# Macaron S4D block on one core: the last two SSM batches made in two parts, by position

## Chip, cores and metric

One core of a Trainium2 chip runs the whole kernel. The metric is device time in microseconds (us) of one execution; the comparison is with the kernel before on the same chip.

## The reference

Input `x` is 8 sequences of 2048 positions with 256 features, all in float32. Three sublayers follow one another:

```python
x = x + 0.5 * ffn(layernorm(x), w1, b1, w2, b2)          # sublayer a
x = x + attn(layernorm(x), ...)                          # the SSM
x = x + 0.5 * ffn(layernorm(x), w1, b1, w2, b2)          # sublayer b, same weights

def ffn(x, w1, b1, w2, b2):       # 256 -> 1024 -> 256
    return relu(x @ w1 + b1) @ w2 + b2

def attn(x, ...):                 # S4D, 256 channels, 64 complex states each
    K = 2 * real(einsum('hn,hnl->hl', Ct, exp(dtA * l)))  # a kernel of 2048 lags
    y = irfft(rfft(x, 2 * L) * rfft(K, 2 * L))[:L]        # causal convolution
    r = x + y + x * D
    return layernorm(r) * ln_w + ln_b
```

## The kernel before

**Tiles.** A sequence is cut into 16 chunks of 128 positions; 8 sequences times 16 chunks are 128 columns (chunk and sequence). The feed-forward sublayers take them two columns at a time, as 64 groups of 256 tokens. After sublayer a the normalized rows lie in one large buffer, `u`, with four quarters `q` of 32 columns each and 256 channels in each quarter. The outputs of the SSM are written back into the same buffer, seen through the view `uo`.

**The SSM.** The convolution is done chunk by chunk: a state per channel, carried from chunk to chunk. The 256 channels are 32 batches of 8 (`bt`), and the batches form ten groups (`PLAN`, L1026) of 2, 4 or 4 batches, whose states lie in one of three buffers, `xsE`, `xsA` and `xsB`. They share their places with the weights: `xsA` with the first weights (tag `wA`), `xsB` with the second (`wB`), `xsE` with tag `wE`. `states` (L1055) makes the chunks' states with the `pt` tables (PE products `pv`, copied out by ACT), `whole` (L1234) carries them over the chunks on DVE, and `outputs` (L1122) makes the rows of a batch:

- SP loads two lag tables `tz` from `kpad` (L1129) and two P tables `ot` (L1147), 256 KB each. Their places rotate by tag, `TZS` and `OTS` (L1034, L1035): even batches in `xl` and `xh`, odd ones in `pl`, `hx`, and the buffer `xn`. For the last group there is a second rotation, in which half of the even batch's tables lie in `x`.
- ACT gathers the batch's channels out of `u` into two tiles `uc` (L1136, tag `hx`).
- PE makes `uc` times `tz` (L1152, 8 products, 16 records in the profile) and the states times `ot` (L1161, 16 products on half the rows each, 32 records), both into two PSUM banks `py`, one for the even and one for the odd channels.
- ACT copies both banks into `uo` (L1167); for the last batch DVE copies the second.

The main loop (L1267) makes a group's outputs and then the states of the group three further on. The last group (`xsE`) holds batches 30 and 31.

**The weights again.** Sublayer a's weights are overwritten by the states, so `again` (L1238) loads them once more for sublayer b: `wb1` as 8 transfers of 256 KB, `wb2` as 4 of 512 KB, on SP. The first four of `wb1` are written down after batch 30's outputs, the others after batch 31's. Each is pinned behind the instruction written just ahead of it on its engine.

**Sublayer b.** `sublayer` (L875) runs over half slots `t`, from -19 on. For t below 0, ACT and DVE keep the order in which the code writes their instructions; after that the library's scheduler orders them by its own estimate, as it does for PE and SP throughout, except where an instruction is pinned. A step of `t` lets each running generator go on to its next `yield`. Each half slot has one block of `up` (PE products `ph`, L856, 6 records), one ReLU on ACT (L928), one difference on DVE (L116) and, three half slots later, one block of `down` (PE products `po`, L866, 6 records). Eight half slots are a group. `pre_b` (L1286) makes a group's input: SP loads `xb`, the rows kept in DRAM (L1293, tag `x`, five places); POOL adds the norm's biases `lnb_sb` (L1294); DVE takes the statistics of the SSM rows (`st_r`), writes (row - mean) times weight into `ys`, scales it and adds it to `xb`; `ffn_in` (L752) takes the statistics again, normalizes into `xn`, transposes (on PE for the first two groups, by DMA for the rest) and splits into `xh` (ACT) and `xl` (DVE). The first groups use the columns of the last quarter, the fourth, and go downwards from there. `post_b` (L1314) adds the result to `xb` on DVE (L1316) and SP stores 256 KB (L1319).

**PSUM banks** (L106): four of tag `h` (`py`, `ph`), two `o` (`pv`, `po`), one `t` and one `b`. SBUF places (L107):

```python
BUFS = {"e": 1, "te": 1, "x": 5, "xh": 2, "xl": 2, "hx": 4, "pl": 2, "g": 1, "gt": 1}
```

Of the kernel before, what the change touches and what calls it, by code (L numbers as in the profile page):

```python
# [10 lines left out]
F32 = mybir.dt.float32  # L11
# [8 lines left out]
P = 128  # L20
# [23 lines left out]
def macaron_s4d_kernel(  # L44
# [17 lines left out]
    nc = tc.nc  # L62
    V = nc.vector
    A_ = nc.scalar
    G_ = nc.gpsimd

    B, L, H = x.shape
    N = c_re.shape[1]
    W = w1.shape[1]
    NJ = L // P  # L70
    CB = (NJ - 1) * B
    NQ = 4
# [3 lines left out]
    NTB = 2  # L76
    TOK = NTB * P
    NG = NJ * B // NTB
# [14 lines left out]
    BCH = 8  # L93
    NBT = H // BCH
    HCH = BCH // 2
    PB = BCH // 2
    KROW = 256
# [6 lines left out]
    wpool = ctx.enter_context(tc.tile_pool(name="wpool", bufs=1))  # L104
# [4 lines left out]
    def bank(tag, name):  # L109
        return ps.tile([P, 512], F32, name=name, tag=tag, bufs=BANKS[tag])  # L110

    def slot(tag, shape, name, dtype=F32):
        return work.tile(shape, dtype, name=name, tag=tag, bufs=BUFS[tag])
# [12 lines left out]
    CQ = JQ * B  # L126
    u = upool.tile([P, NQ, H, CQ], F32, name="u")


    uo = u.rearrange("p q (b h) m -> p q b (h m)", h=8).rearrange("p q b (m h) -> p q b m h", h=8)  # L130
# [84 lines left out]
    o_dram = [dram.tile([P, BCH * P], F32, name=f"o_{i}") for i in range(NBT)]  # L215
    pv_dram = [dram.tile([P, 2 * BCH * P], U16, name=f"pv_{i}") for i in range(2)]
    pt_dram = [dram.tile([P, BCH * P], F32, name=f"pt_{i}") for i in range(NBT)]
    kpad = dram.tile([H, KROW], F32, name="kpad")
# [470 lines left out]
    def stats(srcs, name, pin=False, mv=None):  # L689
        st = stat.tile([P, NTB, 6], F32, name=f"st_{name}", tag="st")  # L690
        mv = moments(NTB, name) if mv is None else mv
        for i, src in enumerate(srcs):
            ins = V.bn_stats(st[:, i, :], src)
            if pin:
                tc.keep_in_program_order(ins)
        for i in range(NTB):
            V.bn_aggr(mv[:, i, :], st[:, i, :])
        return mv
# [329 lines left out]
    sizes = [p[2] - p[1] for p in PLAN]  # L1028
# [2 lines left out]
    SPAN = {"A": 16, "B": 16, "E": 8}  # L1031
    TAGS = ("e", "te")
    LASTX = len(PLAN) - 1
    OTS = ("xh", "xh", "pl", None), ("xh", "x", "pl", None)  # L1034
    TZS = ("xl", "xl", "pl", "hx"), ("xl", "x", "pl", "hx")  # L1035
    xbuf = {}

    def states_of(gr):
        key, at, end = PLAN[gr]
        if key not in xbuf:  # L1040
            t = wpool.tile([P, 2, SPAN[key], NJ * B], F32, name=f"xs{key}", tag=f"w{key}")
            G_.memset(t[:, :, :, 0:B], 0.0)
            xbuf[key] = t
        return xbuf[key][:, :, at:end]

    def batches(gr):
        for p0 in range(0, sizes[gr], PB):
            yield p0, (starts[gr] + p0) // PB
# [54 lines left out]
    def scan(gr, E, p0, p1, j0, j1, tags):  # L1103
# [7 lines left out]
        for j in range(j0, j1):  # L1111
# [7 lines left out]
            E.tensor_add(xv[:, :, :, j + 1, :], xv[:, :, :, j + 1, :], t2)  # L1119
            yield  # L1120

    def outputs(gr, p0, bt):  # L1122
        xs = states_of(gr)
        py, tzs, ucs, ots = [], [], [], []
        for c in range(2):
            tz = slot(TZS[gr >= LASTX][(2 * bt + c) % 4], [P, PB, P], f"tz{bt}_{c}")

            row = kpad[BCH * bt + c, 1:]
            nc.sync.dma_start(  # L1129
                out=tz,  # L1130
                in_=bass.AP(row.tensor, row.offset, [[1, P], [2 * KROW, PB], [1, P]]),
            )
            tzs.append(tz)

            uc = slot("hx", [P, PB, P], f"uc{bt}_{c}")
            A_.copy(  # L1136
                uc.rearrange("p l (q m) -> p l q m", q=NQ),
                u[:, :, BCH * bt + c : BCH * (bt + 1) : 2, :].rearrange("p q l m -> p l q m"),
            )
            ucs.append(uc)  # L1140
        for ri in range(2):
            tag = OTS[gr >= LASTX][(2 * bt + ri) % 4]
            ot = (
                slot(tag, [P, PB, P], f"ot{bt}_{ri}") if tag
                else xn.rearrange("p i (l m) -> p (i l) m", m=P)
            )
            nc.sync.dma_start(out=ot, in_=o_dram[bt][:, ri * PB * P : (ri + 1) * PB * P])  # L1147
            ots.append(ot)
        for c in range(2):
            py.append(bank("h", f"py{bt}_{c}").rearrange("p (l m) -> p l m", l=PB))  # L1150
            for l in range(PB):
                nc.tensor.matmul(  # L1152
                    py[c][:, l, :], ucs[c][:, l, :], tzs[c][:, l, :],
                    start=(l == 0), stop=False, skip_group_check=True,
                )

        for l in range(PB):
            for ri in range(2):
                for c in range(2):
                    cs = slice(c * N, (c + 1) * N)  # L1160
                    nc.tensor.matmul(  # L1161
                        py[c][:, l, :], xs[cs, ri, p0 + l, :], ots[ri][cs, l, :],
                        start=False, stop=(l == PB - 1 and ri == 1), skip_group_check=True,
                    )
        for c in range(2):

            (V.tensor_copy if bt == NBT - 1 and c else A_.copy)(  # L1167
                uo[:, :, bt, :, c::2], py[c].rearrange("p l (q m) -> p q m l", q=NQ)
            )

    def some(j0, j1):

        if (j1 - j0) % JQ == 0:
            return u[:, j0 // JQ : j1 // JQ]
        q = j0 // JQ
        return u[:, q : q + 1, :, (j0 - q * JQ) * B : (j1 - q * JQ) * B]
# [57 lines left out]
    def whole(gr):  # L1234
        for _ in scan(gr, V, 0, sizes[gr], 1, NJ - 1, TAGS):
            pass

    def again():  # L1238

        wb1 = wpool.tile([P, 2, NDC, W], F32R, name="wb1", tag="wA")  # L1240
        for f in range(0, W, W // 4):
            fs = slice(f, f + W // 4)
            for i in range(2):
                tc.keep_in_program_order(
                    nc.sync.dma_start(out=wb1[:, i, :, fs].bitcast(F32), in_=w1_dram[i][:, :, fs])
                )
            if f == W // 4:
                yield
        wb2 = wpool.tile([P, 2, NFC, H], F32R, name="wb2", tag="wB")
        for f in range(0, NFC, 4):  # L1250
            fs = slice(f, f + 4)
            for i in range(2):
                tc.keep_in_program_order(
                    nc.sync.dma_start(out=wb2[:, i, fs].bitcast(F32), in_=w2_dram[i][:, fs])
                )
        yield wb1, wb2

    reload = again()

    for _ in head:  # L1260
        pass
# [1 line left out]
    for _ in states(2):  # L1263
        pass
    whole(2)
    for gr in range(len(sizes)):
        for p0, bt in batches(gr):  # L1267
            outputs(gr, p0, bt)
            if bt == NBT - 2:
                next(reload)  # L1270
        if gr + AHEAD < len(sizes):
            for _ in states(gr + AHEAD):
                pass
            whole(gr + AHEAD)
    wb1, wb2 = next(reload)

    G_.memset(xn[:, :, H - 1 : H], 1.0)
    ys = wpool.tile([P, 2, NTB, H], F32, name="ys", tag="wE")


    lnw_sb = slot("e", [P, H], "lnw_sb")
# [4 lines left out]
    def pre_b(g):  # L1286
        by_dma = g >= DMA_B

        for _ in range(0 if by_dma else (3, 5)[g]):
            yield  # L1290
        xt = xts[g] = slot("x", [P, NTB, H], f"xb_{g}")
        i0 = g * NTB
        nc.sync.dma_start(out=xt, in_=x1_dram[i0 : i0 + NTB].rearrange("i m h -> m i h"))  # L1293
        G_.tensor_add(xt, xt, lnb_sb.unsqueeze(1).to_broadcast([P, NTB, H]))  # L1294
        uc = [uo[:, i // CQ, :, i % CQ] for i in range(P - 1 - i0, P - 1 - i0 - NTB, -1)]
        mv = stats(uc, f"r{g}", PIN & 2)
        yield
        s = root(mv, f"r{g}")
        yield
        y = ys[:, g % 2]  # L1300
        for i in range(NTB):
            yb, lb = (t.rearrange("p (b h) -> p b h", h=BCH) for t in (y[:, i, :], lnw_sb))
            stt(yb, uc[i], mv[:, i, 0:1], lb, ALU.subtract, ALU.mult)
        yield
        rs = rstds(mv, s, f"r{g}")
        yield
        for i in range(NTB):
            ins = stt(xt[:, i, :], y[:, i, :], rs[:, i : i + 1], xt[:, i, :], ALU.mult, ALU.add)
            if PIN & 1:
                tc.keep_in_program_order(ins)  # L1310
        yield
        return (yield from ffn_in(xt, f"b{g}", NTB if g else 1, by_dma))

    def post_b(g, po):  # L1314
        xt = xts.pop(g)
        V.tensor_add(xt, po, xt)  # L1316
        yield
        rows = out[0, g * NTB]
        nc.sync.dma_start(  # L1319
            out=bass.AP(rows.tensor, rows.offset, [[P * H, NJ], [L * H, B], [1, NTB * H]]),  # L1320
            in_=xt.rearrange("p i h -> p (i h)"),
        )

    sublayer(
        [wb1[:, i] for i in range(2)], [wb2[:, i] for i in range(2)], pre_b, post_b, 19, "b"
    )


# [30 lines left out]
```

## Time and profile before

| | |
|---|---|
| median of 3 runs | 1771.14 us (1767.55 to 1773.35) |
| the profiled execution | 1773.44 us |
| its span, first to last instruction | 1771.7 us |
| PE busy | 1728.3 us, 98% of the span |
| DVE busy | 1370.2 us, 77% |
| ACT busy | 997.8 us, 56% |
| POOL busy | 592.8 us, 33% |
| mean granted clock of PE | 0.993 |
| last product of the SSM to first `ph_b` | 1017.2 to 1026.4 us |
| last product of sublayer b | 1767.0 us |

In the profile's lines a time is the start and the number after it the length, in us. `[0.70 <-DMA ot<-o]` says that the engine had stood idle for 0.70 us before the instruction, and that the one that ended it was the transfer of `ot`. PE is TensorE's products and PEld its weight loads, which overlap; DVE is VectorE, ACT ScalarE, POOL GpSimd, and SPq the queue on which SP issues transfers. `py<-tz,uc 128*128 128x128` is a product of a 128 by 128 stationary operand with 128 columns. A float32 product shows as two records; `x16` merges 16 of them. Names end in `_a` or `_b` for the sublayer. Two stretches matter here: about 990 to 1052 us, the seam between the SSM and sublayer b, and the last 5 us.

### The profile page before, as it was taken

The numbers are of one execution on the slowest core, as the hardware profiler recorded it, in microseconds if no ns is written. First come the engines' busy times: TensorE is split into PE (matmuls) and PEld (weight loads), VectorE is DVE, ScalarE is ACT, GpSimd is POOL, SyncE is SP. The second block draws the span as 40 slices with busy tenths as digits, with TensorE's granted clock in tenths as the row PEclk, the third lists the DMA queues.
The fourth block names the chain that finished last, engine by engine and source line by source line (L and its number), as shares of the span: only waits on it lengthen the run. The fifth ranks groups of instructions, "written<-read, shape, count | busy, mean of one in ns | idle before, by whom it ended". The sixth has DMA issues, their size and how long they took to land.

```text
span 1771.7 us, 41027 instructions
## 1 busy us (share of the span) xinstructions
PE 1728.3 (98%) x15347; PEld 1698.5 (96%) x15347; DVE 1370.2 (77%) x4415; ACT 997.8 (56%) x2188; POOL 592.8 (33%) x550
## 2 busy tenths in 40 slices
PE   8999899999999999999999989999999999999998
PEld 7999899999999999998999889999999999999998
DVE  6998877686666666666999788887888888888884
ACT  4554566667777865553555545555555555555553
POOL 1116969966777115111000122222212222222220
PEclk9999999999999999999999989999999999999999
DMA  5111366569877633345898923333333333333331
GB/s 194 43 48 40 77 197 206 180 215 289 233 237 234 201 93 102 96 110 159 255 268 256 285 78 98 91 89 94 90 96 93 93 89 92 92 94 96 90 93 52
DMA packets 299278, 245.31 MB, mean 138 GB/s; under 512 B 169924, under 2 KB 242372, under 8 KB 298566
## 3 DMA queue, kind: packets, MB, share of 16 engines
q1 hardware_dynamic: 297168, 241.23, 46.9%
q8 instruction: 120, 1.97, 0.5%
q0 software_dynamic: 928, 1.19, 0.3%
q14 instruction: 80, 0.66, 0.1%
q10 hardware_dynamic: 982, 0.27, 0.1%
HBM read 91.89 MB, written 111.15 MB: 115 GB/s over the span
## 4 chain that ended last, share of the span: by engine, by line
PE 82%; DMA 7%; DVE 5%; ACT 3%; issue 1%; POOL 0%; SPq 0%; DVEq 0%; ACTq 0%
PE ph_b L856 21%; PE po_b L866 21%; PE ph_a L856 15%; PE po_a L866 15%; PE py L1161 3%; PE py L1152 3%; PE pv L1086 3%; DMA xa<-in_L_attn_x_dram 2%; DMA pt<-pt 1%; DMA planes<-pv 1%; DVE q_u L116 1%; DMA pv<-planes 1%; DVE hx_a L116 1%; PE pt_a L794 1%; ACT u L730 1%
## 5 line engine op out<-in xcount | busy, mean ns | idle before, releaser
L866 PE MATMUL po_a<-wa,hx_a 128*128 128x256 f32 x3072 | 457.4, 286 | 15.1 <-DVE hx_a L116 15.0
L856 PE MATMUL ph_a<-xh_a,wa 128*128 128x256 f32 x2048 | 456.4, 287 | 2.1 <-ACT xh_a L803 1.4
L856 PE MATMUL ph_b<-xh_b,wb 128*128 128x256 f32 x2048 | 443.1, 284 | 0.9 <-ACT xh_b L803 0.7
L866 PE MATMUL po_b<-wb,hx_b 128*128 128x256 f32 x3072 | 441.5, 283 | 0.0
L866 PEld LDWEIGHTS po_a<-wa,hx_a 128*128 128x128 f32 x3072 | 406.9, 193 | 19.0 <-DVE hx_a L116 17.5
L866 PEld LDWEIGHTS po_b<-wb,hx_b 128*128 128x128 f32 x3072 | 400.8, 192 | 0.1
L856 PEld LDWEIGHTS ph_a<-xh_a,wa 128*128 128x128 f32 x2048 | 357.1, 194 | 5.1 <-ACT xh_a L803 1.8
L856 PEld LDWEIGHTS ph_b<-xh_b,wb 128*128 128x128 f32 x2048 | 353.0, 193 | 1.5 <-ACT xh_b L803 1.1
L928 ACT ACTIVATE hx_b<-ph_b 128x256 fp32r<-128x256 f32 x512 | 194.5, 382 | 257.2 <-PE ph_b L856 246.9
L928 ACT ACTIVATE hx_a<-ph_a 128x256 fp32r<-128x256 f32 x512 | 192.7, 386 | 213.1 <-PE ph_a L856 203.9
L116 DVE SCALAR_TENSOR_TENSOR hx_a<-ph_a,hx_a 128x256 fp32r<-128x256 f32 x512 | 208.3, 413 | 128.2 <-ACT hx_a L928 126.6
L856 PE MATMUL ph_a<-xl_a,wa 128*128 128x256 f32 x1024 | 292.5, 287 | 3.6 <-DVE xl_a L837 3.2
L856 PE MATMUL ph_b<-xl_b,wb 128*128 128x256 f32 x1024 | 285.3, 284 | 0.0
L116 DVE SCALAR_TENSOR_TENSOR hx_b<-ph_b,hx_b 128x256 fp32r<-128x256 f32 x512 | 212.1, 415 | 60.5 <-ACT hx_b L928 54.4
L1294 POOL TENSOR_TENSOR xb<-xb,lnb_sb 128x512 f32<-128x512 f32 x64 | 82.6, 1292 | 513.9 <-DMA xb<-x_dram 383.9
L856 PEld LDWEIGHTS ph_a<-xl_a,wa 128*128 128x128 f32 x1024 | 198.9, 194 | 4.8 <-DVE xl_a L837 3.8
L856 PEld LDWEIGHTS ph_b<-xl_b,wb 128*128 128x128 f32 x1024 | 197.6, 193 | 0.1
L777 POOL TENSOR_TENSOR xa<-xa,hb 128x512 f32<-128x512 f32 x64 | 89.1, 1392 | 271.0 <-ACT xn L730 266.0
L777 POOL TENSOR_TENSOR xb<-xb,hb 128x512 f32<-128x512 f32 x64 | 94.9, 1483 | 45.2 <-ACT xn L730 21.7
L730 ACT ACTIVATE xn<-xb,nb_fb,t_fb 128x255 f32<-128x255 f32 x127 | 69.4, 594 | 70.9 <-DVE nb_fb L116 70.9
L815 DVE COPY pl_b<-xn 128x512 uint16<-128x512 uint16 x62 | 43.9, 707 | 74.5 <-ACT xn L730 74.5
L730 ACT ACTIVATE u<-xa,nb_u,t_u 128x256 f32<-128x256 f32 x104 | 90.0, 865 | 0.0
(263 smaller groups left out, 2525.5 us busy)
## 6 DMA issues: line engine op xcount, KB each, us to landing
xa<-in_L_attn_x_dram SPq DMA_DIRECT2D x64, 256.0 KB, 3.1
o<-u SPq DMA_DIRECT2D x32, 512.0 KB, 3.7
pv<-planes SPq DMA_DIRECT2D x32, 512.0 KB, 3.7
pt<-u SPq DMA_DIRECT2D x32, 512.0 KB, 3.8
tz<-kpad SPq DMA_DIRECT2D x64, 256.0 KB, 4.6
xb<-x_dram SPq DMA_DIRECT2D x64, 256.0 KB, 2.7
out_dram<-xb SPq DMA_DIRECT2D x64, 256.0 KB, 3.0
x_dram<-xa SPq DMA_DIRECT2D x62, 256.0 KB, 2.5
```

The lines of the kernel that those rows point to most:

```text
L116: return V.scalar_tensor_tensor(out=o, in0=a, scalar=s, in1=b, op0=op0, op1=op1)
L730: ins = A_.activation(dst, src, AF.Identity, bias=nb[:, i : i + 1], scale=rs[:, i : i + 1])
L777: return G_.tensor_add(xt, xt, hb2.unsqueeze(1).to_broadcast([P, NTB, H]))
L794: nc.tensor.transpose(pt[:, dc * TOK + i * P : dc * TOK + (i + 1) * P], xn[:, i, dc * P : (dc + 1) * P], ident,)
L815: copy(pl[:, w], xu[:, :, :, :, w])
L856: nc.tensor.matmul(ph, wt[wp][:, dc, fs], xp[:, dc, :], start=(n == 0), stop=(n == 3 * NDC - 1))
L866: nc.tensor.matmul(po[:, i, :], hp[:, tsl], wt[wp][:, fc, :], start=(fc == 0 and i == 0 and n == 0), stop=(fc == NFC - 1 and n == 2), skip ...
L928: last[A_] = A_.activation(hh, ph, AF.Relu)
L1086: ins = nc.tensor.matmul(pv[ri][c * N : (c + 1) * N, l, j0 * B : j1 * B], pts[c][:, l, ri * N : (ri + 1) * N], some(j0, j1)[:, :, BCH * bt ...
L1152: nc.tensor.matmul(py[c][:, l, :], ucs[c][:, l, :], tzs[c][:, l, :], start=(l == 0), stop=False, skip_group_check=True,)
L1161: nc.tensor.matmul(py[c][:, l, :], xs[cs, ri, p0 + l, :], ots[ri][cs, l, :], start=False, stop=(l == PB - 1 and ri == 1), skip_group_check ...
L1294: G_.tensor_add(xt, xt, lnb_sb.unsqueeze(1).to_broadcast([P, NTB, H]))
```

## The change

The last two batches, 30 and 31, no longer go through `outputs`. A new function `finish` makes their products in two parts: first for both batches the last quarter of positions (32 of the 128 columns of every table), into two banks that both batches share, copied out in one go by ACT and DVE; then the other three quarters (96 columns) into two `h` banks and two `o` banks. These are copied by ACT in a generator `fetch`, which runs as the first work of sublayer b: after 6 steps the first batch's, after 8 more the second's.

Batch 31's four tables go to four of the five `x` places (`late_tables`), batch 30's to `xl` and `xh`; all eight loads are pinned, 31's first. The second rotation of places goes. `again` no longer stops after four transfers: all 12 come after `finish`. For the first two groups of sublayer b `ys` takes a `pl` place each, and the buffer of tag `wE` is used only from the third on. For the last group `post_b` adds and stores its two columns one after the other, the first through SP and the second through ACT.

```diff
-    OTS = ("xh", "xh", "pl", None), ("xh", "x", "pl", None)
-    TZS = ("xl", "xl", "pl", "hx"), ("xl", "x", "pl", "hx")
+    OTS = "xh", "xh", "pl", None
+    TZS = "xl", "xl", "pl", "hx"
...
+    def load_lags(bt, c, tz, pin=False):
+        row = kpad[BCH * bt + c, 1:]
+        ins = nc.sync.dma_start(
+            out=tz,
+            in_=bass.AP(row.tensor, row.offset, [[1, P], [2 * KROW, PB], [1, P]]),
+        )
+        if pin:
+            tc.keep_in_program_order(ins)
+        return tz
+
+    def load_p(bt, ri, ot, pin=False):
+        ins = nc.sync.dma_start(out=ot, in_=o_dram[bt][:, ri * PB * P : (ri + 1) * PB * P])
+        if pin:
+            tc.keep_in_program_order(ins)
+        return ot
+
+    def gathered(bt, c):
+        uc = slot("hx", [P, PB, P], f"uc{bt}_{c}")
+        A_.copy(
+            uc.rearrange("p l (q m) -> p l q m", q=NQ),
+            u[:, :, BCH * bt + c : BCH * (bt + 1) : 2, :].rearrange("p q l m -> p l q m"),
+        )
+        return uc
...
-            (V.tensor_copy if bt == NBT - 1 and c else A_.copy)(
-                uo[:, :, bt, :, c::2], py[c].rearrange("p l (q m) -> p q m l", q=NQ)
+            A_.copy(uo[:, :, bt, :, c::2], py[c].rearrange("p l (q m) -> p q m l", q=NQ))
+
+    def late_tables():
+        tzs = [load_lags(NBT - 1, c, slot("x", [P, PB, P], f"tz{NBT - 1}_{c}"), True) for c in range(2)]
+        ots = [load_p(NBT - 1, ri, slot("x", [P, PB, P], f"ot{NBT - 1}_{ri}"), True) for ri in range(2)]
+        return tzs, ots
+
+    def finish(late):
+        xs = states_of(LASTX)
+        bts = [bt for _, bt in batches(LASTX)]
+        tzs = [[load_lags(bts[0], c, slot("xl", [P, PB, P], f"tz{bts[0]}_{c}"), True) for c in range(2)]]
+        ots = [[load_p(bts[0], ri, slot("xh", [P, PB, P], f"ot{bts[0]}_{ri}"), True) for ri in range(2)]]
+        tzs.append(late[0])
+        ots.append(late[1])
+        ucs = [[gathered(bt, c) for c in range(2)] for bt in bts]
+
+        def products(n, py, cols, first):
+            for c in range(2):
+                for l in range(PB):
+                    nc.tensor.matmul(
+                        py[c][:, l, :], ucs[n][c][:, l, :], tzs[n][c][:, l, cols],
+                        start=(first and l == 0), stop=False, skip_group_check=True,
+                    )
+            for l in range(PB):
+                for ri in range(2):
+                    for c in range(2):
+                        cs = slice(c * N, (c + 1) * N)
+                        nc.tensor.matmul(
+                            py[c][:, l, :], xs[cs, ri, n * PB + l, :], ots[n][ri][cs, l, cols],
+                            start=False, stop=(l == PB - 1 and ri == 1), skip_group_check=True,
+                        )
+
+        CL = (NQ - 1) * CQ
+        ends = [
+            bank("h", f"pye_{c}")[:, 0 : 2 * PB * CQ].rearrange("p (b l m) -> p b l m", b=2, m=CQ)
+            for c in range(2)
+        ]
+        for n in range(2):
+            products(n, [e[:, n] for e in ends], slice(CL, P), n == 0)
+        for c in range(2):
+            (V.tensor_copy if c else A_.copy)(
+                uo[:, NQ - 1, bts[0] : bts[1] + 1, :, c::2], ends[c].rearrange("p b l m -> p b m l")
+            )
+        rests = []
+        for n in range(2):
+            py = [
+                bank("ho"[n], f"pyr{bts[n]}_{c}")[:, 0 : PB * CL].rearrange("p (l m) -> p l m", l=PB)
+                for c in range(2)
+            ]
+            products(n, py, slice(0, CL), True)
+            rests.append(py)
+        return bts, rests, CQ
+
+    def fetch(bts, rests, CQ):
+        for n, steps in enumerate(FETCH):
+            for _ in range(steps):
+                yield
+            for c in range(2):
+                A_.copy(
+                    uo[:, 0 : NQ - 1, bts[n], :, c::2],
+                    rests[n][c].rearrange("p l (q m) -> p q m l", m=CQ),
+                )
+
+    FETCH = 6, 8
...
-            if f == W // 4:
-                yield
...
-        yield wb1, wb2
-
-    reload = again()
+        return wb1, wb2
...
-    for gr in range(len(sizes)):
+    for gr in range(LASTX):
         for p0, bt in batches(gr):
             outputs(gr, p0, bt)
-            if bt == NBT - 2:
-                next(reload)
...
-    wb1, wb2 = next(reload)
+    rest = fetch(*finish(late_tables()))
+    wb1, wb2 = again()
...
+    def row_sums(g):
+        if g < 2:
+            return slot("pl", [P, NTB, H], f"ys_{g}")
+        if not ys:
+            ys.append(wpool.tile([P, 2, NTB, H], F32, name="ys", tag="wE"))
+        return ys[0][:, g % 2]
...
-        y = ys[:, g % 2]
+        y = row_sums(g)
...
     def post_b(g, po):
         xt = xts.pop(g)
-        V.tensor_add(xt, po, xt)
-        yield
-        rows = out[0, g * NTB]
-        nc.sync.dma_start(
-            out=bass.AP(rows.tensor, rows.offset, [[P * H, NJ], [L * H, B], [1, NTB * H]]),
-            in_=xt.rearrange("p i h -> p (i h)"),
-        )
+        parts = ((0, 1), (1, 2)) if g == NG - 1 else ((0, NTB),)
+        for i0, i1 in parts:
+            V.tensor_add(xt[:, i0:i1], po[:, i0:i1], xt[:, i0:i1])
+            if g < NG - 1:
+                yield
+            rows = out[0, g * NTB + i0]
+            (nc.scalar if i0 else nc.sync).dma_start(
+                out=bass.AP(rows.tensor, rows.offset, [[P * H, NJ], [L * H, B], [1, (i1 - i0) * H]]),
+                in_=xt[:, i0:i1].rearrange("p i h -> p (i h)"),
+            )
 
     sublayer(
-        [wb1[:, i] for i in range(2)], [wb2[:, i] for i in range(2)], pre_b, post_b, 19, "b"
+        [wb1[:, i] for i in range(2)], [wb2[:, i] for i in range(2)], pre_b, post_b, 19, "b",
+        rest,
     )
```

## The prediction

> **What bounds the kernel now.** The profiled execution took 1773.44 us: a span of 1771.7 us and 1.74 us around it. The runs shown have a median of 1771.14 us (1767.55 to 1773.35), so my sum is a difference, taken off that median. I read the shares first (PE 98%), then the chain of waits to find where PE is not fed, then each engine's timeline around those places. PE is full from 1040 us to the end; what the change touches is one seam, from the last products of the SSM to the first rows of sublayer b. PE's timeline there:
>
> ```profile
> 1001.64 0.49 PE L1161 MATMUL py<-ot,xsB 64*128 64x128 f32 x4 [0.70 <-DMA ot<-o]
> 1002.94 1.83 PE L1161 MATMUL py<-ot,xsB 64*128 64x128 f32 x28 [0.81 <-DMA ot<-o]
> ...
> 1012.63 2.05 PE L1152 MATMUL py<-tz,uc 128*128 128x128 f32 x16
> ...
> 1016.78 0.39 PE L1161 MATMUL py<-xn,xsE 64*128 64x128 f32 x4
> 1024.60 1.11 PE L794 MATMUL pt_b<-ident,xn 128*128 128x128 f32 x4 [7.42 <-ACT xn L730]
> 1026.38 1.23 PE L856 MATMUL ph_b<-xh_b,wb 128*128 128x256 f32 x4 [0.68 <-ACT xh_b L803]
> ```
>
> Batch 28 waits 0.70 and 0.81 us for its P tables; after batch 31 (over at 1017.22) PE stands 7.42 us for the norms of sublayer b's first rows, and `ph_b` starts at 1026.38. The table of stretches adds the clock (columns: length, busy time and count of PE, PEld, DVE, ACT, POOL, then granted clock, DMA share, GB/s):
>
> ```profile
> 1020.40:1020.60 0.20, 0.00 (x0) 0.00 (x0) 0.13 (x1) 0.00 (x0) 0.00 (x0) 0.72 1.10 451
> 1030.60:1030.80 0.20, 0.20 (x3) 0.20 (x3) 0.20 (x1) 0.15 (x1) 0.00 (x0) 0.68 0.00 0
> 1026.38:1040.25 13.87, 13.87 (x99) 13.80 (x100) 13.59 (x57) 5.63 (x16) 2.87 (x3) 0.84 0.01 2
> ```
>
> The clock halves about 3.3 us after PE stops and comes back at 1030.7, so the first 4.35 us of `ph_b` run at half speed. But in the same stretch DVE is busy 13.59 of 13.87 us: it is as full as PE. SP's queue and the rows for prices:
>
> ```profile
> 991.76 0.65 SPq L1245 DMA_DIRECT2D wb<-w_dram  x1
> ...
> 999.53 0.33 SPq L1147 DMA_DIRECT2D xn<-o  x1
> 1000.27 0.37 SPq L1129 DMA_DIRECT2D tz<-kpad  x1
> 1004.59 0.32 SPq L1147 DMA_DIRECT2D ot<-o  x1
> ...
> 1012.18 3.45 SPq L1254 DMA_DIRECT2D wb<-w_dram  x4
> ```
> ```profile
> 817.23 9.22 PE L1086 MATMUL pv<-u,pt 128*64 128x96 f32 x256
> 837.74 1.96 PE L1086 MATMUL pv<-u,pt 128*64 128x128 f32 x30 [1.68 <-DMA pt<-pt]
> ```
> ```profile
> L1086 PEld LDWEIGHTS pv<-u,pt 128*64 128x64 f32 x448 | 18.2, 137 | 4.3 <-DMA pt<-pt 2.2 <-ACT xsB L1053 1.1 <-issue 0.6
> L866 PEld LDWEIGHTS po_a<-wa,hx_a 128*128 128x128 f32 x30 | 3.8, 191 | 0.0
> ```
>
> **1, the reload leaves the middle of the SSM.** Four quarter loads of `wb1` (1 MB, from 991.76) no longer run beside batch 28's tables, which took 6.42 us to land. The two waits go: 1.51 us. Batch 29 then ends at 1008.67 - 1.51 = 1007.16.
>
> **2, the tables of batches 30 and 31.** The order is now pinned behind batch 29's last table (999.53): 31's four into `x`, 30's two lag tables into `xl`, 30's two P tables into `xh`, then all 12 reload transfers. An issue takes about 0.6 us (`tz`) and 0.35 (`ot`): 31's are out at 1001.9, 30's lags at 1003.1, 30's P at 1003.9 (their place is free when 28 ends, 1003.2). From issue to landing this stretch has medians of 5.6 (`tz`) and 5.0 (`ot`), at worst 6.4. Second lag table: 1002.5 + 5.6 = 1008.1, first product 1008.4 with a margin for eight transfers at once. PE waits 1.2 us (bounds 0 and 1.7). The P tables (1008.9) come while the lag products run. Before, these batches lost 0.2 us at 1014.7 and 1015.3.
>
> **3, products in two parts.** Each batch has 16 records of `tz` products (1.98 us, 124 ns each) and 32 of `ot` products (1.99 us, two side by side): 32 slots of 124 ns, 7.9 us for two batches. The change makes all of them twice, with 32 and with 96 of 128 columns. No row has 128 wide weights and few columns. Lower bound: 256 `pv` records of 96 and 24 columns by turns took 9.22 us, 72 ns a couple; 128 columns cost 65, so 96 cost 49 and 24 the other 23; two run side by side, so 46 ns a slot. Upper bound: 124, no cheaper. I take 108: a weight load grows from 137 to 191 ns as the weights go from 64 to 128 wide, 54 ns for 64, and every product here still loads 128. The end quarter: 64 slots x 0.108 = 6.9 us (2.9 to 7.9), 1008.4 to 1015.3. The rest, 96 columns: by columns 93, so also 108: 6.9 us (6.0 to 7.9), to 1022.2.
>
> [...] The trace has steady `ph_b` and `po_b` products, 128 wide weights on all rows, every 120 ns, less than a load of 108 and the product in a row, so here loads overlap. [...]
>
> **4, the chain to the first rows.** From 1017.22 to 1026.38 are 9.16 us. The copy on DVE falls from 0.69 to about 0.42 (256 columns; a 256 column DVE operation from PSUM takes 0.42). The transposes take 1.11 at half clock, 0.55 at full: PE now works until 1022.2 and wants the first row at about 1022.4, so the clock stays. 9.16 - 0.27 - 0.56 = 8.3: `ph_b` starts at 1023.6, **2.8 us earlier** (bounds: 1007.2 + 2.9 + 8.3 = 1018.4 gives 8.0; 1008.9 + 7.9 + 8.3, and 0.8 because the rest then ends late, 1025.9 gives 0.5).
>
> **What I cost at nothing, and its cover.** The rest on PE: covered by the norm chain by 0.2 us; past that each us is one on the path. The four copies of the rest on ACT: about 0.5 us each (0.64 for 512); the first two stand in ACT's order ahead of the first rows' second root. They wait for batch 30's rest (1018.8) and end at 1019.9; the root is due at 1015.3 + 5.1 = 1020.4. The other two come after the first `xh` and before the second rows' root, whose reader was due 2.2 us after `ph_b`'s start; about 1.2 are used. The gathers of `u` (0.62 each, ACT) get their `hx` places at 1004.9 and are done at 1006.8. The reload: SP issues it from 1004.3 to about 1012.6; 4.2 MB at 355 GB/s after the tables end at about 1021, `po_b` needs `wb2` at 1027. POOL's loads of the norm's weights and biases take 5.5 us from 1006.86 and are due at 1016.7. `xb` of the second rows now waits for a lag table's place (about 1019), lands behind the reload at 1022.5, POOL adds 1.27, due about 1028. `ys` of the first two lies in `pl`, free at 1007.
>
> **5, the ramp after it.** At full clock PE could do the 13.87 us stretch in 12.1 (16 half slots of 0.72 and the transposes). DVE's list in it stays the same 13.59 us. I take 0.3; bounds 0 and 1.8.
>
> **6, the last rows.** Before: products end at 1767.0, add 0.69 on DVE, DMA 2.8 to landing, end 1771.7. After: two adds of about 0.42, nearly the same end, but only 128 KB left for the last transfer, on ACT's queue. I take 0.3 us less; bounds 0.7 less and 0.5 more, as no row shows ACT's queue this late.
>
> **Sum:** 2.8 + 0.3 + 0.3 = 3.4 us less: 1770.0 against the profiled execution, **1767.7** against the median. Own range: 10.5 less (8.0 + 1.8 + 0.7) to no change.
>
> **Rivals.** (a) Narrow products go by their columns after all: 46 ns slots, end quarter over at 1011.3, `ph_b` at 1019.6, 6.8 + 0.3 + 0.3 = 7.4 less: 1763.7. For it: the 24 column row; against: its weights are 64 wide. (b) The change doesn't do what it says: 124 ns slots and tables at their latest, so the end quarter is over only 0.4 us before the whole was, and 0.5 is gained at `ph_b`: 1770.6. For it: 124 ns for every product of this kind seen. (c) Slower: `xb` of the first rows goes behind the reload in SP's queue. Before, its three loads went at 973.85 into free `x` places; now four of five are the tables', the fifth is given after them, and the reload is pinned right there. It would land at 1022 (355 GB/s) to 1025.8 (274); POOL's add ends 1.3 later and `ph_b` follows 5.6 after that, at 1028.9 to 1032.7: with the last rows' 0.3 off, 2.2 to 6.0 more, **1775.2** in the middle. It decides from a landing after about 1016.7; from 1020 the whole gain is gone. Against it: SP has a pause before 30's P tables, into which the load fits.
>
> **How the numbers follow.** Forecast 0.38, (a) 0.32, (b) 0.10, (c) 0.20. About 0.3% (5.3 us) is what a measurement can tell from no change. Faster by more: (a), and the 0.06 of the forecast in which PE also gets much of the ramp, 0.38. Slower by more: 0.14, the part of (c) near its late end, as tables and reload then share the DMA engines. Within: the other 0.48. The forecast's likely range is 1765 to 1770; with (a) and (c) the range is 1762 to 1775.5.
>
> **What would show it.** Step 1: no wait of batch 28 for `ot`. Step 2: a wait of 0 to 1.7 us ahead of batch 30's first product. Step 3: the spacing of the 32 column products, 46 or 108 ns. Step 4: no 7.4 us gap and clock 1.00 from 1017 to 1030. Step 5: DVE still over 95% busy for the first rows. Step 6: the time from the last product to the end against 4.7 us. I am wrong if `xb` of the first rows is issued after the reload, or if PE waits at the second or third rows for their `xh`.

## The result, and the profile after

The changed kernel takes **1781.52 us** (median of five runs, 1779.16 to 1786.71) against 1771.14: ratio **1.0067 [1.0051, 1.0082]**, slower, where 1767.7 was forecast. The profiled execution took 1786.0 us, a span of 1784.2: 12.5 us more than the 1771.7 of before. PE's timeline at the seam (start, length, operation, idle time before it):

```profile
1000.30 2.05 PE L1165 MATMUL py<-tz,uc 128*128 128x128 f32 x16
...
1007.17 3.34 PE L1202 MATMUL pye<-tz,uc 128*128 128x32 f32 x16 [2.84 <-DMA tz<-kpad]
1010.44 3.63 PE L1210 MATMUL pye<-ot,xsE 64*128 64x32 f32 x32
...
1021.11 3.73 PE L1202 MATMUL pyr<-tz,uc 128*128 128x96 f32 x16
...
1032.08 3.73 PE L1210 MATMUL pyr<-ot,xsE 64*128 64x96 f32 x32
1035.75 1.11 PE L794 MATMUL pt_b<-ident,xn 128*128 128x128 f32 x4
1037.54 1.23 PE L856 MATMUL ph_b<-xh_b,wb 128*128 128x256 f32 x4 [0.67 <-ACT xh_b L803]
```

Batch 29 flows through without a wait and ends at 1004.33. Then PE stands 2.84 us for batch 30's first lag table. And then the surprise: half of a batch's whole products takes 2.05 us (first line), but half of a batch at *a quarter of the columns* takes 3.63, and with 96 columns 3.73. The 7.42 us hole ahead of `pt_b` is gone, because PE is busy right up to it. The table of stretches says why (length; busy time and count of PE, PEld, DVE, ACT, POOL; then granted clock, DMA share, GB/s):

```profile
1004.30:1007.20 2.90, 0.06 (x3) 0.06 (x1) 0.00 (x0) 1.11 (x2) 0.00 (x0) 1.00 1.10 296
1007.20:1009.00 1.80, 1.80 (x10) 1.80 (x11) 0.00 (x0) 0.00 (x0) 0.00 (x0) 0.57 1.05 371
1014.00:1017.50 3.50, 3.50 (x18) 3.48 (x16) 0.00 (x0) 0.00 (x0) 0.00 (x0) 0.50 1.05 392
1028.40:1032.00 3.60, 3.60 (x18) 3.49 (x16) 2.02 (x10) 1.68 (x4) 0.65 (x1) 0.50 0.10 27
1042.00:1044.00 2.00, 1.73 (x15) 1.55 (x14) 2.00 (x8) 0.84 (x3) 0.00 (x0) 1.00 0.02 4
```

The clock halves at 1007.45, just as PE starts again (1007.17), and then **stays at 0.50 for 34 us, with PE busy for all but 0.7 of them**; it comes back near 1041.6, some 4 us after the 256 column products of `ph_b` begin. Before, it was half from 1020.5 to 1030.7, and for 4.8 us of that PE had nothing to do.

Where 12.5 us of span went, by four points of the two timelines:

| stretch | before | after | difference |
|---|---|---|---|
| start to the end of batch 29 | 1008.67 | 1004.33 | -4.34 |
| to the first `ph_b` | 17.71 | 33.21 | **+15.50** |
| to the last product | 740.6 | 742.4 | +1.8 |
| to the end | 4.70 | 4.26 | -0.44 |

Of the 4.34, 1.51 are the two waits of batch 28. Another 2.56 were there before that batch began (its first product starts at 996.33 against 998.89), where the two programs are alike: that is what one execution differs from another. A slot, here and below, is the time from one record of a product on 128 rows to the next (on 64 rows, where two run side by side, 32 records in 2.06 us against 16 in 2.05, from one pair of records to the next). The 33.21 are 2.84 of pause, 13.95 for 64 slots of 32 columns (218 ns each), 14.64 for 64 slots of 96 (229 ns), and 1.78 from there to `ph_b`.

The queue of SP, for the rival in which `xb` goes behind the reload:

```profile
1001.94 0.76 SPq L1374 DMA_DIRECT2D xb<-x_dram  x1
...
1004.27 6.64 SPq L1322 DMA_DIRECT2D wb<-w_dram  x8
```

The first rows' `xb` is issued ahead of the reload. And the last rows: both adds on DVE, then the second transfer from ACT's queue:

```profile
1780.04 0.76 DVE L1400 TENSOR_TENSOR xb<-po_b,xb 128x256 f32<-128x256 f32 x2 [2.10 <-PE po_b L866]
```
```profile
1780.88 0.66 ACTq L1404 DMA_DIRECT2D out_dram<-xb  x1
```

### The profile page after: what moved, and what is told of

It reads as the page before. It is cut to its first block, busy times and chain, and to the rows that moved or that the text cites. A ratio compares the mean times of both kernels' runs of the same rounds, so it can differ in the third digit from the quotient of the medians.

```text
span 1784.2 us, 41222 instructions
## 1 busy us (share of the span) xinstructions
PE 1749.2 (98%) x15443; PEld 1720.3 (96%) x15443; DVE 1370.0 (77%) x4416; ACT 996.9 (56%) x2190; POOL 593.2 (33%) x550
## 4 chain that ended last, share of the span: by engine, by line
PE 86%; DVE 5%; DMA 4%; ACT 2%; issue 1%; POOL 1%; SPq 0%; DVEq 0%; ACTq 0%; POOLq 0%
PE ph_b L856 21%; PE po_b L866 20%; PE ph_a L856 16%; PE po_a L866 16%; PE py L1174 3%; PE py L1165 3%; PE pv L1086 3%; DMA xa<-in_L_attn_x_dram 2%; DVE q_u L116 1%; DMA pt<-pt 1%; DVE hx_a L116 1%; PE pt_a L794 1%; DMA planes<-pv 1%; DVE st_fa L693 1%; ACT hx_a L928 0%
```

## The experiments

Two explanations had to be told apart first. **The pause**: a PE that stood for 2.84 us loses its clock and runs on at half. **The narrow products**: PE loses its clock, or can't get it back, because of what it is fed. Behind both stood a third question, whether two parts could have paid at any clock. All ratios are against the kernel before, run on the same chip; "early" means that the tables of batch 31 are asked for before the outputs of the group ahead of the last.

| run | what it is | ratio |
|---|---|---|
| e1_early | the change, early tables, no pause at batch 30 | 1.0078 [1.0056, 1.0101] |
| e2_fill | the change, the pause filled with products | 1.0070 [1.0047, 1.0093] |
| e3_whole | the change, products whole | 1.0020 [1.0006, 1.0035] |
| e4_whole_early | products whole, early tables | 1.0012 [1.0002, 1.0022] |
| e5_early_dense | e1, second part 128 columns wide | 1.0049 [1.0030, 1.0067] |
| e6_rest_first | e1, the 96 columns first | 1791.63 us, one run |
| e7_warm | before, its hole filled | 1.0000 [0.9986, 1.0015] |
| e8_copy_tail | before, copy split, last rows split | 0.9990 [0.9978, 1.0002] |
| e9_copy_tail_late | e8, reload behind batch 31 | **0.9971 [0.9959, 0.9984]** |
| e10_whole30 | whole, batch 30's tables first, copy split | 1.0053 [1.0034, 1.0072] |
| e11_whole30_xb | e10, `xb` ahead of the reload | 0.9991 [0.9980, 1.0001] |

### e1_early: no pause

```diff
     for gr in range(LASTX):
+        if gr == LASTX - 1:
+            late = late_tables()
...
-    rest = fetch(*finish(late_tables()))
+    rest = fetch(*finish(late))
```

> The changed kernel with one move: batch 31's four tables are asked for before batch 26's outputs, so that batch 30's are first in SP's queue behind batch 29's. Theory 1 (the pause of 2.84 us ahead of batch 30 halves the clock, and the narrow products only fail to bring it back): the pause falls under 1 us, the clock stays at 1.00 from 1000 us to the first ph_b, the end quarter takes about 6.9 us and the rest about 6.9 instead of 14.0 and 14.6, and the time is 1766 to 1771 us. Theory 2 (the narrow products themselves let the clock fall, pause or none): the clock falls to 0.50 some 3 to 7 us after the first narrow product, both parts together take 22 to 28 us, and the time is 1776 to 1782 us.

PE's timeline and stretches of e1:

```profile
1007.61 1.97 PE L1202 MATMUL pye<-tz,uc 128*128 128x32 f32 x16
```
```profile
1008.00:1012.00 4.00, 4.00 (x53) 3.92 (x52) 0.00 (x0) 0.83 (x2) 1.31 (x2) 1.00 1.08 367
1012.00:1014.00 2.00, 2.00 (x23) 1.96 (x22) 0.00 (x0) 0.00 (x0) 0.00 (x0) 0.91 1.10 354
1014.00:1016.00 2.00, 2.00 (x22) 2.00 (x21) 0.00 (x0) 0.00 (x0) 0.00 (x0) 0.50 1.05 391
```

The products start without a wait and at full clock: this is their true price, 1.90 us for 16 slots (start to start), **119 ns a slot where whole ones take 124**. And then, 6 us in (the mean of 0.91 puts it at about 1013.6), the clock halves with PE 100% busy and no gap in the 20 us before. The pause isn't needed for it. It wasn't gone either: it had moved to batch 26 (1.67 us at 991.0; the 16 products behind it took 2.02 us, so the clock was full), since the tables asked for early now stand ahead of that batch's in SP's queue. The time is no better than the change's.

### e2_fill: the pause filled

```diff
+        fill_ = bank("b", "fill")
+        for _ in range(14):
+            tc.keep_in_program_order(
+                nc.tensor.matmul(fill_[:, 0:P], ident, ident, start=True, stop=True)
+            )
```

> The changed kernel with its tables as late as they are, but 14 products of the identity with itself (128 columns, results not used) on PE right behind batch 29, 3.5 us at full clock, so that PE does not stand while it waits. Theory 1 (pause): clock 1.00 until the first ph_b, the two parts about 13.8 us together, 1768 to 1772 us. Theory 2 (narrow products): clock 0.50 from some us into the end quarter, 1777 to 1783 us. Together with the run before: if only one of the two holds the clock, neither theory is enough.

The stretches of e2, from the filling products (1008.17 to 1011.4) on:

```profile
1008.00:1011.40 3.40, 3.40 (x34) 3.26 (x31) 0.00 (x0) 1.14 (x2) 0.00 (x0) 1.00 1.03 303
1011.40:1014.00 2.60, 2.23 (x22) 2.13 (x20) 0.00 (x0) 0.00 (x0) 0.28 (x1) 1.00 1.07 366
1014.00:1016.00 2.00, 1.45 (x16) 1.34 (x15) 0.00 (x0) 0.00 (x0) 1.02 (x2) 0.58 1.09 350
```

PE's timeline where it falls:

```profile
1013.82 0.41 PE L1210 MATMUL pye<-ot,xsE 64*128 64x32 f32 x4 [0.37 <-DMA ot<-o]
1014.78 3.20 PE L1210 MATMUL pye<-ot,xsE 64*128 64x32 f32 x28 [0.55 <-DMA ot<-o]
```

Full through the pause, and gone 3 us into the narrow products: the mean of 0.58 puts it at 1014.3. That is inside the second of two short waits for P tables, 0.37 and 0.55 us, so e2 isn't as clean as e1, where PE never stood. The end is the same by another way: the pause only decides a few us of when.

### e3_whole and e4_whole_early: the same places and pins, products whole

```diff
-            products(n, py, slice(0, CL), True)
-            rests.append(py)
+            products(n, py, slice(0, P), True)
+            for c in range(2):
+                (V.tensor_copy if n and c else A_.copy)(
+                    uo[:, :, bts[n], :, c::2], py[c].rearrange("p l (q m) -> p q m l", q=NQ)
+                )
```

with the part for the end quarter taken out, and in e4 the early tables of e1.

> The changed kernel with all its tables, places and pins, but the products of batches 30 and 31 made whole, 128 columns, and copied out whole as before. The pause ahead of batch 30 stays (about 2.8 us), so the clock should fall here too. If it is the narrow columns that keep it down (theories 1 and 2), the 128 column products bring it back after 3 to 7 us: 64 slots take 10 to 12 us, the gap to the first rows is 7 us again, 1771 to 1775 us. Theory 3 (no float32 product brings the clock back, only sublayer b's): 64 slots of 228 ns, 14.6 us, 1777 to 1780 us.

> The changed kernel with whole 128 column products and with batch 31's tables asked for early: everything of the change but the split, and no pause. If the split alone is what costs, this stands at the kernel before or a little under it: clock 1.00 over the two batches (7.9 us), no wait of batch 28 (1.5 us less), a gap of 7.4 us to the first rows as before, the end 0.4 us shorter: 1 to 2 us under the kernel before. If the places of the tables, the late reload or ys cost something too, it is slower than before by what they cost.

PE's timeline of e3, and its stretches:

```profile
1010.38 3.49 PE L1202 MATMUL pyw<-tz,uc 128*128 128x128 f32 x16 [2.62 <-DMA tz<-kpad]
1013.80 2.06 PE L1210 MATMUL pyw<-ot,xsE 64*128 64x128 f32 x32
```
```profile
1010.40:1012.00 1.60, 1.60 (x7) 1.60 (x8) 0.00 (x0) 0.00 (x0) 0.00 (x0) 0.50 1.08 394
1012.00:1014.00 2.00, 2.00 (x12) 1.88 (x13) 0.00 (x0) 0.00 (x0) 0.97 (x1) 0.63 1.08 359
1014.00:1016.00 2.00, 2.00 (x34) 1.88 (x32) 0.00 (x0) 0.06 (x1) 0.33 (x2) 1.00 1.09 346
```

The same pause, the same fall to 0.50, but whole products have the clock back after 3 us. So a pause costs some 2.6 us plus 1.4 for the slow start, and the cut of the products costs the rest: e1 against e4, which differ in it and its copies alone, 1.0078 to 1.0012, is 0.66%, 11 to 12 us; the change against e3, 1.0067 to 1.0020, about 8. These intervals don't meet. e3 and e4 have their 7.5 and 8.5 us holes ahead of `pt_b` again, and are still faster than the change that filled it. e4 misses its own expectation, about 2 us over the kernel before in place of 1 to 2 under it: its early tables cost a wait of 2.48 us at batch 26, and the 16 products right behind that wait took 3.30 us where others of their kind take 2.05.

### e5_early_dense and e6_rest_first: which width does what

In e5 the second part runs over all 128 columns, the last 32 of them a second time, and 96 are copied out:

```diff
-            products(n, py, slice(0, CL), True)
+            products(n, py, slice(0, P), True)
```

In e6 the block of the 96 columns stands ahead of the block of the 32. Both have the early tables.

> e1_early with the second part made over all 128 columns, of which 96 are used (the last 32 are computed twice). [...] Theory B (once down, the clock only comes back with sublayer b's products, or it hangs on the repeated weight loads): 14.6 us again, time as e1_early.

> e1_early with the order turned round: the 96 column part first, from a full clock, then the end quarter. Only the clock and the spacing are of interest. [...] If 1.00 holds over the 7.6 us of the 96 column part, that part alone would have been harmless and the end quarter is what spoils it; if it falls within 3 to 7 us, both parts are at fault. In the end quarter it falls in any case.

PE's timeline of e5, whose clock had fallen among the 32 column products, at 1017.5:

```profile
1025.27 3.78 PE L1202 MATMUL pyr<-tz,uc 128*128 128x128 f32 x16
1028.98 3.10 PE L1210 MATMUL pyr<-ot,xsE 64*128 64x128 f32 x32
```

The second line's 3.10 is half slow, half fast: 128 columns have the clock back after 6 us, at 1031.2, and the second part takes 10.7 us instead of 14.6, so theory B fell. e5 computes more than e1 and is 5 us faster by its median, though the two intervals overlap by 0.1%. PE's timeline of e6, with the 96 columns first:

```profile
1019.86 2.03 PE L1210 MATMUL pyr<-ot,xsE 64*128 64x96 f32 x32
...
1023.72 1.98 PE L1210 MATMUL pye<-ot,xsE 64*128 64x32 f32 x32
1025.63 2.08 PE L1202 MATMUL pye<-tz,uc 128*128 128x32 f32 x16
```

From a full clock, 96 columns keep it for all of their 7.8 us (122 ns a slot), and it goes 5.5 us into the 32 columns (these begin at 1021.82), at about 1027.4. So 96 columns hold a full clock, and in the 14.6 us of the change and of e1 they don't restore a half one. A rival cause, the traffic of the DMA engines beside PE, falls with the same rows: in e6 their share was 1.02 to 1.11 while the clock held (stretches of 2 us from 1014 to 1024) and 0.16 in the two us in which it fell (1026 to 1028), and in the change it was 0.00 from 1021.5 to 1027 with the clock at 0.50.

### e7_warm: was the half clock of before worth anything?

```diff
+    warm_ = bank("b", "warm_")
+    for _ in range(28):
+        tc.keep_in_program_order(
+            nc.tensor.matmul(warm_[:, 0:P], ident, ident, start=True, stop=True)
+        )
```

> The kernel before with 28 products of the identity with itself (128 columns, not used) on PE behind batch 31, 6.9 us in the 7.4 us gap: the clock should stay at 1.00 from the SSM into sublayer b. Tests the ramp by itself. If DVE sets the ramp (as the prediction took it), ph_b to the second group still takes 13.5 to 14 us and at most 0.7 us are gained, the transposes' 0.5 among them. If the half clock sets it, 12.1 us and 2 to 2.7 us gained.

In the ramp of e7, from the first `ph_b` on:

```profile
1021.50:1035.40 13.90, 12.70 (x100) 12.07 (x100) 13.49 (x48) 5.48 (x15) 4.06 (x4) 1.00 0.00 1
```

The clock is full, and from the first `ph_b` to the second group (1021.48 to 1035.44) are 13.96 us where before had 14.06. PE now idles 1.2 us of it, and DVE is busy for 13.49 of 13.90. Nothing was to be had there: ratio 1.0000.

### e8_copy_tail and e9_copy_tail_late: the good parts on the kernel before

e8 keeps whole products and copies batch 31's last quarter first (one bank on ACT, one on DVE), then the rest; it also has the change's last rows. e9 moves the reload behind batch 31 as well:

```diff
+        for q0, q1 in ((NQ - 1, NQ), (0, NQ - 1)) if bt == NBT - 1 else ():
+            for c in range(2):
+                (V.tensor_copy if c and q0 else A_.copy)(
+                    uo[:, q0:q1, bt, :, c::2],
+                    py[c][:, :, q0 * CQ : q1 * CQ].rearrange("p l (q m) -> p q m l", m=CQ),
+                )
...
-            if bt == NBT - 2:
+            if bt == NBT - 1:
                 next(reload)
```

> The kernel before with two edits: batch 31's copies take the last quarter of positions first (ACT and DVE, 128 columns each) and the rest after it on ACT, so that the COPY is split and no product is made twice; and the last rows end one by one as in the change. The first rows' statistics should start about 0.4 us earlier after the last product and the end be 0.4 us shorter: 0.8 us under the kernel before, which five rounds can hardly tell. If it is slower, splitting costs something even without the narrow products.

> e8_copy_tail with the whole reload of the weights behind batch 31's tables instead of four transfers in the middle. If the prediction's first step holds (the two waits of batch 28, 1.5 us, come from those four transfers), it is 1 to 2.3 us under the kernel before. If the reload only moves the waits, it equals e8.

PE's timeline of e8, then of e9:

```profile
997.20 0.49 PE L1161 MATMUL py<-ot,xsB 64*128 64x128 f32 x4 [1.71 <-DMA ot<-o]
```
```profile
1018.23 1.11 PE L794 MATMUL pt_b<-ident,xn 128*128 128x128 f32 x4 [7.02 <-ACT xn L730]
```

The hole is 7.02 instead of 7.42 us in both. e8's waits in batch 28 (1.71 and another 0.18 us) are gone in e9: from the first product of batch 26 to that of batch 31 are 22.40 us in e8 (985.17 to 1007.57) and 19.83 in e9 (986.86 to 1006.69). e8 can't be told from no change. **e9 is faster than both kernels**, 1770.21 against 1775.20 on its chip, about 5 us. That is more than the 1 to 2.3 us expected; its profile accounts for the 2.57 and for the small gains that it shares with e8. The intervals of e8 and e9 overlap by 0.06%, so the step between these two rests on the rows rather than on the times.

### e10_whole30 and e11_whole30_xb: the places of the change without its pause

e10 keeps the change's places, asks for batch 30's tables before 31's, and has whole products and the split copy. e11 also issues `xb` by hand:

```diff
     rest = finish(None)
+    xts[0] = slot("x", [P, NTB, H], "xb_0")
+    tc.keep_in_program_order(
+        nc.sync.dma_start(out=xts[0], in_=x1_dram[0:NTB].rearrange("i m h -> m i h"))
+    )
     wb1, wb2 = again()
```

> The changed kernel with whole products, batch 30's tables asked for ahead of 31's (all behind batch 29's last), and batch 31's copies split as in e8. The pause ahead of batch 30 should fall under 1 us, with no wait of batch 26 or 28; the clock stays at 1.00 until the gap. Everything of the change without the narrow products and without the pause: 1 to 2.5 us under the kernel before; if the late second rows' xb or the tables cost something, as much as before.

> The kernel of e10 (whole products, batch 30's tables ahead of batch 31's), with one edit: the load of the first rows' xb is issued by hand ahead of the weights' reload. In e10's profile it was issued at 1014.45, behind the reload (1003.09 to 1014.0), its add on GpSimd began at 1022.8, and the first transpose waited 18.39 us for the norm. Theory 1 (the late xb is what e10 lost by): the transposes wait 7 to 7.5 us as in the other kernels with whole products, so ph_b starts 11 us earlier (at about 1021) and the time falls from e10's 1.0053 to a ratio of about 0.999 (0.997 to 1.001). Theory 2 (the reload itself, by crowding the DMA engines, holds up the tables and the x1 rows): xb lands little sooner, the wait stays over 12 us and the ratio above 1.003. Theory 3 (the clock, since e10's gap of 18 us halved it): the same fall of the wait, but the ramp after it shows the clock, not xb, was worth most: the time from ph_b to the loop's second group, not the wait, changes by over 2 us.

SP's queue and PE's timeline of e10:

```profile
1003.09 7.18 SPq L1315 DMA_DIRECT2D wb<-w_dram  x8
...
1014.45 3.88 SPq L1367 DMA_DIRECT2D xb<-x_dram  x5
```
```profile
1030.61 1.11 PE L794 MATMUL pt_b<-ident,xn 128*128 128x128 f32 x4 [18.39 <-ACT xn L730]
```

The last products ran through without a wait and at full clock until 1012.2, and all of it is lost again: the reload is issued first and `xb` behind it, GpSimd's add begins at 1022.8, and the transposes wait 18.39 us. (That it is the missing wait for batch 30's places in SP's queue that lets the reload go first is argued from the order of the issues, not tried.) In e11:

```profile
1005.17 0.48 SPq L1342 DMA_DIRECT2D xb<-x_dram  x1
1005.76 7.97 SPq L1315 DMA_DIRECT2D wb<-w_dram  x8
```
```profile
1021.44 1.11 PE L794 MATMUL pt_b<-ident,xn 128*128 128x128 f32 x4 [7.09 <-ACT xn L730]
```

11 us of wait gone and 0.6% of the time: theory 1 holds. From `ph_b` to the second group are then 16.23 us against e10's 13.58, and PE waits three times in them for `hx_b` from DVE (0.43, 0.20 and 0.47 us; in e10 not once). The second rows' `xb` still goes behind the reload (issued at 1017.03), so GpSimd's next adds now fall into this stretch (the first at 1025.33). In e10 they began at 1022.8, and the pair of DVE operations that stood beside them (`xb<-ys,t_r,xb`, at 1024.05) took 2.87 us, which takes 0.88 in the kernel before. That GpSimd's adds slow DVE's is a guess from their standing side by side. The longer stretch eats 2.65 of the 11, and at 1052.0, in the second group, PE waits another 2.36, for `xh`.

## Why the prediction was wrong

**1, right.** No wait of batch 28: the 1.51 us are gone, and e9 gains by it without the rest of the change (2.57 us in its profile, against e8).

**2, too small.** 2.84 us of wait instead of 1.2, beyond the bound of 1.7: batch 30's lag tables landed 7.2 us after their issue, where 5.6, at worst 6.4, was taken (31's, issued ahead of them, took 5.0). 31's tables, `xb` and the reload were beside them on the DMA engines (share 1.10 in those 2.9 us); that these held them up is likely, and was not tried alone.

**3 and 4, the step that failed.** The sum had 108 ns a slot and, in step 4, "so the clock stays". The price itself was mis-sized a little: 119 ns for 32 columns (e1), 122 for 96 (e6), 124 for whole ones, with loads and products overlapping (from 1008 to 1012 in e1 PEld was busy for 3.92 of 4.00 us and PE for all of them). The clock was the error: it was 0.50 where the step needed 1.00. At half clock the end quarter took 13.95 us instead of 6.9 and the rest 14.64 instead of 6.9. At the full-clock prices both would be 64 x 0.119 + 64 x 0.122 = 15.4, so 13.2 us are the clock's, more than the whole loss. That a busy PE keeps a full clock is what the kernel before shows for its own products, of 128 columns (1.00 from 1005 to 1010) and of 256 (1.00 from 1032 to 1040); the prediction noted that no row showed 128 wide weights with few columns, and bounded their price for it, but not the clock. For 32 columns it doesn't hold: e1 has no gap in the 20 us before its clock halves.

The cover of the rest then turned into the bound. The prediction had it 0.2 us inside the norm chain, "past that each us is one on the path": it went 4.5 us past (the first `xn` was there at 1031.3, PE was free at 1035.75). The copies of the rest on ACT, costed at nothing, held up the first rows' root by 3.29 us besides, as they stand ahead of it and waited for those products; PE was later still, so it cost nothing.

Even at full clock nothing much was to be won. Every product is made twice, and a narrow slot costs nearly what a whole one does: 15.4 us instead of 7.9 fill a hole of 7.4 with 7.5 us of extra work. With 1.3 us of transposes and split (1.34 at full clock in e5), `ph_b` would come 16.7 us after batch 29 without any pause; before needed 17.7. This is worked out, not measured: no run held the clock through the narrow products.

**5, right in the mechanism.** The ramp is DVE's: 14.06 us before, 13.96 with a full clock (e7), 14.3 in the change, so the 0.3 taken for it was 0.1 at most. **6, right:** 4.26 us from the last product to the end, 0.44 less where 0.3 was taken.

**The rivals.** (a), slots by columns, fell: 119 ns at 32. (b) had the nearest prices, 124 ns and late tables, but kept the clock as well, and so missed the time as the forecast did. (c) isn't what happened: `xb` went out at 1001.94, in SP's pause for batch 30's P tables, as the argument against it said. It is real all the same: in e10, without that pause, the transposes wait 18.39 us instead of 7.42, and the run is about 9 us slower than the kernel before, more than the 2.2 to 6.0 it was given. The sign was thus right for a rival whose mechanism wasn't at work, and no case had the clock in it. A wait at the second or third rows for their `xh`, named as a sign of error, didn't come: PE's one long wait in the ramp was 1.47 us at 1064.5, for `hx` from DVE, most of the +1.8.

**What stays open.** Why the clock wants more than 32 columns: the runs show that it depends on the width of the products, not what is counted. Columns streamed in a given time would fit all of it: at full clock 32 in 119 ns lose it, 96 in 122 keep it; at half clock 96 in 229 ns don't bring it back, 128 in 232 do. That is a guess that fits; no width between 32 and 96 was tried, and no other load at the same rate.

## What to carry to other kernels

Before cutting a product's free dimension, price the slot, not the columns: with a fresh 128 wide operand each time, a slot of 32 float32 columns costs 119 ns and one of 128 costs 124, so two parts are twice the work. Read the granted clock in the rows of the very shape you will issue; a busy PE is no proof of a full clock (0.50 with PE busy for 2.00 of 2.00 us in e1, 1014 to 1016). When only an early piece of a result is wanted, split the copy and not the product, and look in the queue for what the freed order now lets ahead of the next stage's first load.

## What the hardware showed that was not expected

- With PE busy without a gap, the clock fell from 1.00 to 0.50 after 6 us (e1) and 5.5 us (e6) of 32 column float32 products.
- 96 columns held 1.00 for 7.8 us (e6) and stood at 0.50 for 14.6 us (after); 128 columns brought it back in 3 us (e3) and 6 us (e5).
- The delays need not be a property of the widths. In the traces of before and after, every stretch at half clock that begins and ends inside the trace lasts 3.41, 10.24 or 34.13 us, whole multiples of 3.41, and the stretches at full clock between them are such multiples too (10.24 before and 34.13 after are the ones at the seam). By the mean clock in stretches of 2 and 4 us, others at the seam are 3.4 us (e3, around its pause), 13.6 (e5) and 23.9 (e1). Counted back 3.41 us from a change of the clock, an estimate from these times, the time ahead of it held 32 column products alone where it fell in e1 (1010.23 to 1013.64) and e6 (1023.95 to 1027.36), and 128 column products alone where it came back in e5 (1027.79 to 1031.20). That the clock is decided in such steps was not shown.
- Short pauses cost clock as well: behind waits of 2.40 us (batch 26 in e6) and 2.48 (batch 26 in e4) the next 16 products took 3.34 and 3.30 us where others of their kind take 2.05, and around the end of one of 2.62 (e3) the clock stood at 0.50 for 3.4 us; behind 1.67 (e1) and 1.73 (e5) they took 2.02.
- The change's five runs show it in their mean clock, 0.985 to 0.990, where the profile of before had 0.993.
